# The hidden state's transposed, normalized copy: loaded and normalized in place instead of transposed on TensorE

## The chip, the cores and the metric

The kernel runs on one core of a Trainium2 chip. The metric is the device time of one execution in microseconds (us); the kernel before has a median of 1011.7 us over three runs (1010.71 to 1012.34).

## What is computed

One gated cross-attention block with a mixture feed-forward, in float32, for 8 batches of 256 tokens of width 512. In short:

```python
x = x + tanh(g_xattn) * attn(layernorm(x), ctx)   # q from [ctx, ln(x)], k and v from ln(x), ssm_k and ssm_v from ctx
x = x + tanh(g_ffn)   * ffn(layernorm(x))         # top-4 router over 128 experts, 8 gated bases, one shared expert
```

`layernorm` subtracts the mean of a token's 512 values and divides by the root of their variance + 1e-5. Queries, keys and values are matmuls that contract over the 512 features, so TensorE wants the normalized hidden state with the features on the partitions: x^T, 512 x 256 per batch, kept as a tile `xnT` of 128 partitions x 4 feature chunks x 256 tokens. The context `ctx` needs no norm and is already handed to the chip transposed.

## The kernel before, in words

**Rounds.** The work of a batch has three parts, and each round runs three batches side by side: `feed_forward(b)` of batch b, `attention(b + 1)` and `project(b + 2)` (the queries, keys and values). After the attention of a half (128 tokens) a `tail` does the output projection, the second norm, its transposes and the router. In the trace a full round takes about 121.8 us; rounds 0 to 5 hold a `project` of batches 2 to 7, and the last two rounds hold none.

**Who sets the order.** Nothing is reordered by hardware or a scheduler: every engine runs its instructions in the order in which Python issues them. Each part is a generator; `yield c` says "the next step of mine is due c units later", and `run` (L1251) always continues the generator that is due first. A round is 1.0 of this planned time. `project(b + 2)` starts at b + 0.01 (batch 2 at -0.06) and 60 of its units are 0.62 of a round (L1283), so one unit is 0.0103 round, nominally 1.26 us. `feed_forward(b)` starts at b, and 72.9 units are a round. `attention(b + 1)` starts at b - 0.2, and 74.1 units are 0.86 of a round.

**The feed-forward's pieces.** It goes through ten pieces of weights (8 bases, 2 shared). A piece is four groups of matmuls into a rotation of three PSUM banks: `one_and_five`, `four` of the piece before, `seven_and_six`, `two_and_three`, with the evictions between them on VectorE (DVE) and ScalarE (ACT): `first_tile` (L1084, L995), `mix_product` (L1113), `second_gate` (L1096), `keep_seven` (L1071 to L1075). Each group, once issued, loads the weights of the piece after next into the buffer that it has freed (`load_gu`, L349 and L351, on SyncE's queue, SP).

**The attention's steps.** `score` (L652) fills four PSUM banks; DVE adds the position bias and takes the row's bound (`soften`, L665); ACT takes exponentials (L684); GpSimd (POOL) divides (`divide`, L696); DVE transposes 32 x 32 blocks (`turn`, L709); TensorE multiplies by the values (L731). A later `score` reuses the four banks, so it follows the last `soften` on them.

**`project(b)` before.** It issues the loads of x and of the transposed context on SP (L112, L118; x has three buffers, so x of batch b waits until the result of batch b - 3 has been written out from the same buffer, L1183). 16 units later `norm` puts two `bn_stats`/`bn_aggr` pairs and an addition on DVE (L179 to L182) and one `pow` on POOL (L184); 3 units later DVE writes the two normalized tiles `xn` (L190); 3 units later the transposes begin. For each half of the tokens, `transposed` (L199) puts four 128 x 128 transposes on TensorE (L204) into the PSUM bank named `one`, and ACT copies them into `xnT` (L205). The bank `one` is shared with the tails: `hold` and `give` (L97 to L105) let one user in at a time, in the order of asking, with a gap of 0.007 round. Then come the keys (L532), the four query groups (L586) and the values (L606), each through the same bank. The tile `xnT` shares two buffers with the attention's `oT`. Batches 0 and 1 are projected by other code, with transposes.

Of the kernel before, what the change touches and what calls it, by code (L numbers as in the profile page):

```python
# [9 lines left out]
F32 = mybir.dt.float32  # L10
I32 = mybir.dt.int32
AF = mybir.ActivationFunctionType
ALU = mybir.AluOpType
AX = mybir.AxisListType

P = 128
B, T, HID = 8, 256, 512
NT = T // P
NC = HID // P
# [12 lines left out]
LN_EPS, EPS = 1e-5, 1e-8  # L32
# [5 lines left out]
def gated_block(  # L38
    ctx: ExitStack,
    tc: tile.TileContext,  # L40
    x: bass.AP,
    context_t: bass.AP,
    g_xattn: bass.AP,
    g_ffn: bass.AP,
# [17 lines left out]
    nc = tc.nc  # L62

    const = ctx.enter_context(tc.tile_pool(name="const", bufs=1))
    one = ctx.enter_context(tc.tile_pool(name="one", bufs=1))
    two = ctx.enter_context(tc.tile_pool(name="two", bufs=2))
    three = ctx.enter_context(tc.tile_pool(name="three", bufs=3))
    four = ctx.enter_context(tc.tile_pool(name="four", bufs=4))
    small = ctx.enter_context(tc.tile_pool(name="small", bufs=4))
# [4 lines left out]
    sums = ctx.enter_context(  # L74
        tc.tile_pool(name="sums", bufs=1, space=bass.MemoryType.DRAM)
    )
# [10 lines left out]
    def other_bank(n, name):  # L87
        return ps_gu.tile([P, 2 * T], F32, tag=f"gu{n}", name=name)
# [8 lines left out]
    def hold(gap=GAP):  # L97
        me = object()
        queue.append(me)
        while queue[0] is not me or now[0] < given[0] + gap:  # L100
            yield 0.4
# [6 lines left out]
    loaded = {}  # L108

    def load(b, eng=nc.sync):  # L110
        xt = three.tile([P, NT, HID], F32, tag="x", name=f"x_{b}")
        eng.dma_start(xt, x[b].rearrange("(t p) d -> p t d", p=P))  # L112
        return xt

    def load_context(b, eng=nc.sync):

        ctT = one.tile([P, NC, T], F32, tag="shT" if b == 1 else "ctT", name=f"ctT_{b}")
        eng.dma_start(ctT, context_t[b].rearrange("(c p) t -> p c t", p=P))  # L118
        return ctT
# [29 lines left out]
    neghalf = const.tile([P, NT], F32, tag="neghalf", name="neghalf")  # L149
# [23 lines left out]
    def norm(xt, tiles, name):  # L173

        n = len(tiles)
        stats = small.tile([P, NT, 6], F32, tag="stats", name=f"st_{name}")
        mv = small.tile([P, NT, 2], F32, tag="mv", name=f"mv_{name}")
        for j, t in enumerate(tiles):
            nc.vector.bn_stats(stats[:, j, :], xt[:, t, :])  # L179
            nc.vector.bn_aggr(mv[:, j, :], stats[:, j, :])  # L180
        veps = small.tile([P, NT], F32, tag="veps", name=f"ve_{name}")
        nc.vector.tensor_scalar(veps[:, :n], mv[:, :n, 1], LN_EPS, None, op0=ALU.add)  # L182
        rstd = small.tile([P, NT], F32, tag="rstd", name=f"rs_{name}")
        nc.gpsimd.tensor_tensor(rstd[:, :n], veps[:, :n], neghalf[:, :n], ALU.pow)  # L184

        def normed():
            xns = []
            for j, t in enumerate(tiles):
                xn = two.tile([P, HID], F32, tag="xn", name=f"xn_{name}_{t}")
                nc.vector.tensor_scalar(  # L190
                    xn, xt[:, t, :], mv[:, j, 0:1], rstd[:, j : j + 1],
                    op0=ALU.subtract, op1=ALU.mult,
                )
                xns.append(xn)
            return xns

        return normed

    def transposed(dst, src, t, name, bank):  # L199


        pt = bank([P, NC, P], f"tr_{name}_{t}")
        for c in range(NC):
            nc.tensor.transpose(pt[:, c, :], src[:, c * P : (c + 1) * P], ident)  # L204
        return lambda: nc.scalar.copy(dst[:, :, t * P : (t + 1) * P], pt)  # L205
# [127 lines left out]
    }  # L333

    summed = set()

    def load_gu(i, g):

        b, k = divmod(i, PIECES)
        if b >= B:  # L340
            return
        wgu[i, g] = ts = [
            two.tile([P, 2, I], F32, tag=f"w{g}{j}", name=f"w{g}{j}_{i}")
            for j in range(1 if g == 3 else 2)
        ]
        if g != 3 or k not in summed:
            of_bases, of_shared = ((w_gate, sw_gate), (w_up, sw_up))[(g - 1) // 2]
            src = of_bases[k] if k < NK else of_shared[k - NK]
            nc.sync.dma_start(ts[0], src[int(g in (2, 4))])  # L349
        if k in summed:  # L350
            nc.sync.dma_start(ts[-1], scratch[k, g])  # L351
# [16 lines left out]
    AFTER, BEFORE = 1.8, 0.8  # L368
# [132 lines left out]
    def put_values(pv):  # L501
# [2 lines left out]
            pv.rearrange("p t s (k d) -> p (t s) k d", d=D),  # L504
        )

    def project(b, xns=None):
        def own():
            yield from hold(0.0 if b == 1 else GAP)

        def bank(shape, name):
            return ps_one.tile(shape, F32, tag="one", name=name)

        free = give
        if b > 1:
            while b > 2 and b - 3 not in stored:
                yield 0.5
            loaded[b] = load(b), load_context(b)
            yield 16.0
        xt, ctT = loaded[b]  # L520
        if xns is None:
            normed = norm(xt, range(NT), f"a{b}")
            yield 3.0
            xns = normed()
            yield 3.0
        xnT = two.tile([P, NC, T], F32, tag="xo", name=f"xnT_{b}")
        kT = two.tile([P, 2, 2, T], F32, tag="kT", name=f"kT_{b}")

        def keys(pk, s):
            w_sb, src = ((wsk_sb, ctT), (wk_sb, xnT))[s]  # L530
            for c in range(NC):
                nc.tensor.matmul(  # L532
                    pk[:, s, :], lhsT=w_sb[:, c, :], rhs=src[:, c, :],
                    start=(c == 0), stop=(c == NC - 1),
                )

        if b == 1:

            yield BEFORE
            yield from own()  # L540
            pk = bank([P, 2, T], f"pk_{b}")
            for t in range(NT):
                if t:
                    yield BEFORE
                    keys(pk, 0)
                    yield MORE
                evict = transposed(
                    xnT, xns[t], t, f"x{b}",
                    lambda shape, name: other_bank(2, name).rearrange("p (c n) -> p c n", n=P),
                )  # L550
                yield AFTER
                evict()
            yield BEFORE
            keys(pk, 1)
            yield AFTER
        else:
            for t in range(NT):
                yield from own()
                evict = transposed(xnT, xns[t], t, f"x{b}", bank)
                yield AFTER - 0.8  # L560
                evict()
                free()
                yield BEFORE + 0.8
            yield from own()
            pk = bank([P, 2, T], f"pk_{b}")
            for s in range(2):
                keys(pk, s)
                yield AFTER

        for par in range(2):  # L570
            for s in range(2):
                nc.scalar.activation(
                    kT[:, par, s, :], pk[:, s, :], AF.Copy, scale=kmask[:, par : par + 1],
                )
        free()
        yield BEFORE
        if b == 1:
            yield BEFORE


        qT = two.tile([P, NB, G, Q], F32, tag="qT", name=f"qT_{b}")
        for g in range(G):
            yield from own()
            pq = bank([P, T], f"pq_{b}_{g}")
            for c in range(2 * NC):
                nc.tensor.matmul(  # L586
                    pq, lhsT=wq_sb[:, c, g * P : (g + 1) * P],
                    rhs=(ctT if c < NC else xnT)[:, c % NC, :],
                    start=(c == 0), stop=(c == 2 * NC - 1),
                )  # L590
                if c % NC == NC - 1:
                    yield MORE if c < NC else AFTER
            nc.scalar.activation(
                qT[:, :, g, :], pq.rearrange("p (b q) -> p b q", q=Q), AF.Copy, scale=-0.25
            )
            free()
            yield BEFORE
        projected[b] = kT, qT


        yield from own()
        pv = bank([P, NT, 2, HK * D], f"pv_{b}")
        for t in range(NT):
            for s, (w_sb, src) in enumerate(((wsv_sb, ctT), (wv_sb, xnT))):
                for c in range(NC):
                    nc.tensor.matmul(  # L606
                        pv[:, t, s, :], lhsT=src[:, c, t * P : (t + 1) * P], rhs=w_sb[:, c, :],
                        start=(c == 0), stop=(c == NC - 1),
                    )
            yield AFTER if t else MORE  # L610
        put_values(pv)
        free()
        yield BEFORE
# [671 lines left out]


_INS = [
    "x", "ctx_2048", "g_xattn", "g_ffn",
    "L0_xattn_Wq", "L0_xattn_Wk", "L0_xattn_Wv", "L0_xattn_Wsk", "L0_xattn_Wsv", "L0_xattn_Wo",
    "L0_ffn_w_router", "L0_ffn_w_gate", "L0_ffn_w_up", "L0_ffn_w_down",  # L1290
    "L0_ffn_amplitudes", "L0_ffn_expert_scale",
# [32 lines left out]
```

## Time and profile before

| | us |
|---|---|
| median of the runs | 1011.7 (1010.71 to 1012.34) |
| the profiled execution's own time | 1013.49 |
| its span in the trace | 1011.7 |
| mean granted TensorE clock | 0.993 |
| one full round (rounds 1, 2, 4, 5) | 121.7 to 121.8 |

The span is what the trace covers; the 1.8 us to the profiled execution's own time lie around it. Where the text speaks of a "view", it is one answer of the trace: the page with its busy shares; the groups (instructions by line, with count and mean duration); the timeline (instructions in order of start); the waits (who waited for whom); the chain of waits that ended last; and the busy time by stages, given by window. In the timeline the first column is the start and the second the time that the merged instructions span, both in us; a bracket gives the idle time before and what ended it. Matmuls are pipelined, so what a group costs TensorE is read from start to start, not from its busy time.

Other groups that are in play, from the same profile:

| line, engine | what | count | mean ns |
|---|---|---|---|
| L204 PE, tr_x | transposes of the hidden state, all batches | 64 | 289 |
| L205 ACT, xnT | their eviction | 16 | 583 |
| L190 DVE, xn_a | normalization, 128 x 512 | 16 | 571 |
| L179 DVE, st_a | statistics, 128 x 512 | 16 | 674 |
| L184 POOL, rs_a | power, 128 x 2 | 7 | 858 |
| L112 SP | load of x, 512 KB, six times | 6 | 4.8 us to landing |
| L118 SP | load of the context, 512 KB | 7 | 5.9 us to landing |

### The profile page before, as it was taken

How to read it: one execution, taken by the hardware profiler on the slowest of the kernel's cores; microseconds unless marked ns; L12 is line 12 of the kernel's file. 1: busy time of each engine (PE TensorE's matmuls, PEld its weight loads, DVE VectorE, ACT ScalarE, POOL GpSimd, SP SyncE). 2: the span in 40 equal slices, each digit the busy share in tenths (PEclk: the TensorE clock that was granted, in tenths of full speed). 3: DMA queues.
4: the chain of work that ended last, by engine and by line, in shares of the span. 5: the costliest groups of instructions: out<-in, count | busy, mean ns of one | idle time of the engine just before them, and what ended most of it. 6: DMA issues, size and time to landing. Idle time of an engine off the chain costs nothing.

```text
span 1011.7 us, 27844 instructions
## 1 busy us (share of the span) xinstructions
PE 985.7 (97%) x10470; PEld 797.3 (79%) x10470; DVE 601.8 (59%) x2241; ACT 441.6 (44%) x1657; POOL 471.6 (47%) x892
## 2 busy tenths in 40 slices
PE   8899799899999999999999999999999999999998
PEld 8777687768888687886778868797788868787885
DVE  2775767467553685536755467645756466665453
ACT  3754444246442564325543356423554245442231
POOL 4783676536542363423634246432455325651341
PEclk9999899999999999999999999999999999999999
DMA  6945744689354784457745586446954468665891
GB/s 208 219 171 155 224 152 129 185 216 304 124 164 144 208 288 142 147 166 217 249 127 158 167 256 216 135 137 190 276 188 140 150 181 260 201 192 167 281 301 64
DMA packets 117302, 192.15 MB, mean 190 GB/s; under 512 B 12848, under 2 KB 34864, under 8 KB 117168
## 3 DMA queue, kind: packets, MB, share of 16 engines
q1 hardware_dynamic: 112672, 184.87, 59.6%
q10 hardware_dynamic: 4112, 4.46, 1.3%
q8 instruction: 83, 1.36, 0.6%
q0 software_dynamic: 384, 1.05, 0.5%
q14 instruction: 51, 0.42, 0.1%
HBM read 158.87 MB, written 14.68 MB: 172 GB/s over the span
## 4 chain that ended last, share of the span: by engine, by line
PE 86%; DVE 5%; issue 2%; ACT 2%; POOL 2%; DMA 1%; SPq 1%; ACTq 0%; DVEq 0%; POOLq 0%
PE m L1028 39%; PE m L1037 10%; PE pq L586 8%; PE sc L731 6%; PE po L893 5%; PE sc L652 5%; PE pd L1171 4%; PE pk L532 2%; PE pv L606 2%; PE pd L1174 2%; PE pl L923 1%; DVE pr L665 1%; ACT pr L684 1%; PE tr_x L204 1%; SPq L496 1%
## 5 line engine op out<-in xcount | busy, mean ns | idle before, releaser
L696 POOL TENSOR_SCALAR pr<-pr,rd 128x192 f32<-128x192 f32 (+2 forms) x512 | 212.1, 434 | 243.9 <-DVE rd L693 226.8
L684 ACT ACTIVATE pr<-pr,nm 128x192 f32<-128x192 f32 (+2 forms) x512 | 219.0, 431 | 106.7 <-DVE nm L665 55.3
L1028 PE MATMUL m<-w,sT 128*128 128x256 f32 x1024 | 252.3, 380 | 1.3 <-issue 0.8
L1028 PEld LDWEIGHTS m<-w,sT 128*128 128x128 f32 x1024 | 193.6, 190 | 28.9 <-issue 1.5
L665 DVE CUSTOM_DVE_ANT_1 pr<-sc,nbias 128x192 f32<-128x192 f32 (+2 forms) x512 | 153.7, 321 | 98.0 <-PE sc L652 91.1
L1028 PE MATMUL m<-w,hT 128*128 128x256 f32 x768 | 203.8, 388 | 1.0 <-DVE u L1073 1.0
L1028 PEld LDWEIGHTS m<-w,hT 128*128 128x128 f32 x768 | 139.6, 191 | 25.6 <-issue 6.3
L1118 POOL TENSOR_TENSOR mixed<-mixed,th 128x256 f32<-128x256 f32 x112 | 81.5, 728 | 137.5 <-DVE th L1113 137.5
L709 DVE STREAM_TRANSPOSE pt<-pr 128x768 f32<-128x768 f32 (+2 forms) x128 | 111.4, 870 | 3.8 <-POOL pr L696 3.1
L684 ACT ACTIVATION_READ_ACCUMULATOR pr<-pr,nm 128x1 f32 x512 | 98.0, 191 | 0.0
L1074 POOL TENSOR_TENSOR m<-m,u 128x256 f32<-128x256 f32 x80 | 61.4, 768 | 67.3 <-DVE u L1073 58.5
L990 ACT ACTIVATE th<-m 128x256 f32<-128x256 f32 x80 | 30.7, 384 | 138.5 <-DVE up L1084 138.4
L731 PEld LDWEIGHTS sc<-pt,vbd 64*32 64x32 f32 x5120 | 60.6, 106 | 25.8 <-issue 14.2
L731 PE MATMUL sc<-pt,vbd 64*32 64x64 f32 (+2 forms) x5120 | 68.2, 228 | 8.9 <-DVE nm L665 5.3
L1096 DVE TENSOR_TENSOR gate<-u,m 128x256 f32<-128x256 f32 x80 | 33.2, 416 | 72.0 <-PE m L1028 66.5
L1084 DVE TENSOR_TENSOR up<-u,m 128x256 f32<-128x256 f32 x80 | 33.3, 416 | 67.9 <-PE m L1028 41.1
L990 ACT ACTIVATE th<-gate 128x256 f32<-128x256 f32 x80 | 33.3, 416 | 76.5 <-DVE gate L1096 76.5
L652 PE MATMUL sc<-kT,qT 32*128 32x192 f32 (+2 forms) x1024 | 63.6, 336 | 2.8 <-DVE nm L665 2.5
L1037 PE MATMUL m<-sT,w 128*128 128x128 f32 x512 | 66.2, 278 | 0.0
L652 PEld LDWEIGHTS sc<-kT,qT 32*128 32x128 f32 x1024 | 44.3, 184 | 26.5 <-issue 7.1
L1037 PEld LDWEIGHTS m<-sT,w 128*128 128x128 f32 x512 | 62.3, 194 | 0.4
L1171 PE MATMUL pd<-sd,shT 128*128 128x512 f32 x128 | 61.5, 603 | 0.2 <-DVE shT L1107 0.2
(131 smaller groups left out, 1376.0 us busy)
## 6 DMA issues: line engine op xcount, KB each, us to landing
w<-s SPq DMA_DIRECT2D x284, 256.0 KB, 3.5
w<-in_L_ffn_w_gate SPq DMA_DIRECT2D x130, 256.0 KB, 3.1
w<-in_L_ffn_w_up SPq DMA_DIRECT2D x73, 256.0 KB, 4.1
vbd<-vpad SPq DMA_DIRECT2D x120, 128.0 KB, 3.1
s<-w SPq DMA_DIRECT2D x40, 256.0 KB, 3.3
w<-in_L_ffn_shared_w_gate SPq DMA_DIRECT2D x32, 256.0 KB, 2.9
w<-in_L_ffn_shared_w_up SPq DMA_DIRECT2D x18, 256.0 KB, 3.8
sd<-in_L_ffn_shared_w_down SPq DMA_DIRECT2D x16, 256.0 KB, 3.5
```

The costliest lines, as they stand in the source:

```text
L586: nc.tensor.matmul(pq, lhsT=wq_sb[:, c, g * P : (g + 1) * P], rhs=(ctT if c < NC else xnT)[:, c % NC, :], start=(c == 0), stop=(c == 2 * N ...
L652: nc.tensor.matmul(seen(scs[p][:, j * COLS : (j + 1) * COLS], qb), lhsT=qT[rows, qb].rearrange("p g q -> p (g q)"), rhs=kT[rows, par, :, f ...
L665: nc.vector.tensor_tensor_reduce(out=part, in0=seen(scs[p][:, j * COLS : (j + 1) * COLS], qb0 + j), in1=bass.AP(tensor=bias.tensor, offset ...
L684: nc.scalar.activation(part, part, AF.Exp, bias=nmax, scale=-1.0, accum_out=den)
L696: nc.gpsimd.tensor_scalar(part, part, rden[:, p : p + 1], 1.0, op0=ALU.mult, op1=ALU.mult)
L709: nc.vector.transpose(pt[:, u % 4].rearrange("p c (s k) -> p (c s) k", s=2)[:, :, lo:], pr.rearrange("p c (s k) -> p (c s) k", s=2)[:, :, ...
L731: nc.tensor.matmul(scs[gp][32 * c : 32 * (c + 1), 2 * COLS + lo * Q : 2 * COLS + hi * Q], lhsT=vbd[rows, kb % (P // Q), kb // (P // Q) * 2 ...
L990: nc.scalar.activation(th, gate, AF.Tanh, scale=0.5)
L1028: nc.tensor.matmul(dst, lhsT=sides_of[m][c], rhs=w[:, c, :], start=(first and c == 0), stop=(c == NC // 2 - 1), skip_group_check=True,)
L1037: nc.tensor.matmul(dst[:, cols], lhsT=w[:, c, cols], rhs=sides_of[m][c], start=(first and ic == c == 0), stop=(c == NC // 2 - 1), skip_gro ...
L1118: nc.gpsimd.tensor_add(mixed[t], mixed[t], th)
L1171: nc.tensor.matmul(po, lhsT=shT[:, ic, t * P : (t + 1) * P], rhs=down[ic], **flags)
```

## The change

From batch 2 on, x is handed to the kernel a second time, transposed on the host. `xnT` is loaded with the raw x^T and normalized where it lies. The mean and the reciprocal deviation of a token are now needed along the free axis, the same on every partition; they are computed as before from x, written to a small DRAM tile `rows` (4-byte elements, 2 KB in all), and read back with a broadcast to all 128 partitions (`wide`, 256 KB). Then DVE subtracts the mean and POOL multiplies, in two halves of 128 x 512 each. The planned distances are new as well: 9 units from the loads to the statistics, 2 to the write, 8 to the read, 8 to the first half, and 2.1 after each half. The transposes, their evictions, and their two turns at the bank `one` are gone for batches 2 to 7. The scratch space for DMAs issued by POOL is set to 8192 bytes.

```diff
+    rows = {b: sums.tile([NT, 2, P], F32, tag=f"rows{b}", name=f"rows{b}") for b in range(2, B)}
...
+    def norm_transposed(b, xt, xnT):
+        stats = small.tile([P, NT, 6], F32, tag="stats", name=f"st_a{b}")
+        mr = small.tile([P, NT, 2], F32, tag="mv", name=f"mv_a{b}")
+        for t in range(NT):
+            nc.vector.bn_stats(stats[:, t, :], xt[:, t, :])
+            nc.vector.bn_aggr(mr[:, t, :], stats[:, t, :])
+        veps = small.tile([P, NT], F32, tag="veps", name=f"ve_a{b}")
+        nc.vector.tensor_scalar(veps, mr[:, :, 1], LN_EPS, None, op0=ALU.add)
+        nc.gpsimd.tensor_tensor(mr[:, :, 1], veps, neghalf, ALU.pow)
+        yield 2.0
+        nc.sync.dma_start(rows[b].rearrange("t s p -> p (t s)"), mr.rearrange("p t s -> p (t s)"))
+        yield 8.0
+        wide = one.tile([P, NT, 2, P], F32, tag="wide", name=f"wide_{b}")
+        nc.sync.dma_start(
+            wide.rearrange("p t s n -> p (t s n)"),
+            rows[b].rearrange("t s p -> (t s p)").partition_broadcast(P),
+        )
+        yield 8.0
+        for half in range(2):
+            part = xnT[:, half * NC // 2 : (half + 1) * NC // 2, :].rearrange(
+                "p c (t n) -> p c t n", t=NT
+            )
+            for which, eng, op in ((0, nc.vector, ALU.subtract), (1, nc.gpsimd, ALU.mult)):
+                row = wide[:, :, which, :]
+                eng.tensor_tensor(
+                    part, part,
+                    bass.AP(
+                        tensor=row.tensor, offset=row.offset,
+                        ap=[list(row.ap[0]), [0, NC // 2], [2 * P, NT], [1, P]],
+                    ),
+                    op,
+                )
+            yield 2.1
...
     def project(b, xns=None):
...
             loaded[b] = load(b), load_context(b)
-            yield 16.0
-        xt, ctT = loaded[b]
-        if xns is None:
-            normed = norm(xt, range(NT), f"a{b}")
-            yield 3.0
-            xns = normed()
-            yield 3.0
-        xnT = two.tile([P, NC, T], F32, tag="xo", name=f"xnT_{b}")
+            xnT = two.tile([P, NC, T], F32, tag="xo", name=f"xnT_{b}")
+            nc.sync.dma_start(xnT, x_t[b].rearrange("(c p) t -> p c t", p=P))
+            yield 9.0
+            xt, ctT = loaded[b]
+            yield from norm_transposed(b, xt, xnT)
+        else:
+            xt, ctT = loaded[b]
+            xnT = two.tile([P, NC, T], F32, tag="xo", name=f"xnT_{b}")
...
-            for t in range(NT):
-                yield from own()
-                evict = transposed(xnT, xns[t], t, f"x{b}", bank)
-                yield AFTER - 0.8
-                evict()
-                free()
-                yield BEFORE + 0.8
             yield from own()
             pk = bank([P, 2, T], f"pk_{b}")
...
-    nc = bacc.Bacc("TRN2", target_bir_lowering=False, num_devices=1)
+    nc = bacc.Bacc(
+        "TRN2", target_bir_lowering=False, num_devices=1, dynamic_dma_scratch_size=8192
+    )
...
-        if name == "ctx_2048":
+        if name in ("ctx_2048", "x_t"):
             a = a.transpose(0, 2, 1)
```

## The prediction

> **What bounds the kernel.** First the page's busy shares, then the busy time by stages, for round 2 (348.3 to 470.1).
>
> ```profile
> PE 985.7 (97%) x10470; PEld 797.3 (79%) x10470; DVE 601.8 (59%) x2241; ACT 441.6 (44%) x1657; POOL 471.6 (47%) x892
> ```
>
> ```profile
> core 0: us, PE busy (x) PEld busy (x) DVE busy (x) ACT busy (x) POOL busy (x), PEclk, DMA share, GB/s
> 348.30:470.10 121.80, 121.47 (x1303) 98.39 (x1299) 72.58 (x278) 55.01 (x206) 52.62 (x103) 1.00 0.61 188
> ```
>
> ```profile
> 355.40:364.60 9.20, 9.20 (x177) 7.61 (x176) 6.49 (x28) 5.44 (x22) 4.62 (x10) 1.00 0.99 351
> 364.60:373.70 9.10, 9.09 (x60) 7.47 (x59) 9.00 (x35) 5.67 (x23) 6.15 (x11) 1.00 0.91 293
> 373.70:382.50 8.80, 8.80 (x113) 7.46 (x112) 5.78 (x25) 4.48 (x18) 6.62 (x13) 1.00 0.49 160
> ```
>
> TensorE is the bound: busy 121.47 of 121.80 us, clock 1.00, and the chain of waits that ended last lies 86% on it. Matmul time taken away is gained in full, unless an engine beside it is late. In 355 to 374 two are near their limit: the DMA engines (0.99, 351 GB/s) and DVE (9.00 of 9.10 us).
>
> **Removed on TensorE.** The timeline of round 2 shows what four transposes cost from start to start.
>
> ```profile
> 371.58 0.60 PE L204 MATMUL tr_x<-ident,xn_a 128*128 128x128 f32 x4
> 372.02 1.03 PE L1028 MATMUL m<-w,hT 128*128 128x256 f32 x4
> 373.06 0.65 PE L204 MATMUL tr_x<-ident,xn_a 128*128 128x128 f32 x4
> 373.65 0.60 PE L652 MATMUL sc<-kT,qT 32*128 32x192 f32 x7
> ```
>
> The first four take 372.02 - 371.58 = 0.44. The four L1028 behind them need 0.86 (the same form goes from 369.86 to 370.72), so TensorE is free for the second four at 372.88 and is done with them at 373.65: 0.77, of which 0.17 are put down to DVE. I count 0.44 + 0.60 = 1.04 per batch; 0.44 + 0.77 = 1.21 is the most, 2 x 0.44 = 0.88 the least. In round 0 the pairs start at 121.93, 122.37 and 125.05, 125.55: 0.94. Five rounds and that: 5 x 1.04 + 0.94 = **6.1 us gained** (5.3 to 7.0).
>
> The Trainium skill speaks against the change here: "VectorE: DVE Perf Modes", The three transpose paths, gives TensorE 390 ns for a 128 x 128 transpose (bf16) and warns of a DMA that transposes by strides. By that figure 48 transposes would be an estimated 18.7 us, three times what the starts show; I go by the starts. The strided DMA is not at issue for x, which the host transposes; no run here shows it.
>
> **Moved: the statistics.** This is the step I fear. One unit is 0.62/60 = 0.0103 round. Before, the statistics stand at 0.01 + 16 x 0.0103 = 0.175 round, now at 0.01 + 9 x 0.0103 = 0.103. In the feed-forward's units that is 0.103 x 72.9 = 7.5. Adding its yields, `mix_product(0, 0)` stands at 1.73 + 1.73 + 0.6 + 1.13 + 0.6 + 1.13 = 6.92 and `second_gate(0)` at 7.78; the attention's steps (0.0116 round each from -0.2) put a `soften` and a `turn` at 0.102. So on DVE the statistics now stand behind the `turn` at 357.35 and ahead of the gate at 358.48. The check on this arithmetic: 0.175 gives 12.8, behind the `silu2` at 11.84, and there the trace has them (364.18).
>
> ```profile
> 354.51 0.38 SPq L112 DMA_DIRECT2D x<-in_x  x1
> ```
>
> The view of L112 in this window gives its landing, and the timeline the DVE instructions (those between are left out):
>
> ```profile
> DMA to landing us min/median/max: 4.8/4.8/4.8
> ```
>
> ```profile
> 357.35 0.44 DVE L709 STREAM_TRANSPOSE pt<-pr 128x256 f32<-128x256 f32 x1
> 358.48 0.42 DVE L1096 TENSOR_TENSOR gate<-u,m 128x256 f32<-128x256 f32 x1 [0.69 <-PE m L1028]
> ...
> 362.96 0.42 DVE L1084 TENSOR_TENSOR up<-u,m 128x256 f32<-128x256 f32 x1 [0.99 <-PE m L1028]
> ...
> 363.57 0.35 DVE L665 CUSTOM_DVE_ANT_1 pr<-sc,nbias 128x192 f32<-128x192 f32 x1
> ...
> 364.18 0.69 DVE L179 BATCH_NORM_STATS2 st_a<-x 128x6 f32<-128x512 f32 x1
> ```
>
> The load of x is not earlier: on SP it waits for the result of batch b - 3 to leave its buffer. It lands at 354.51 + 4.8 = 359.3, but DVE gets to the statistics at 357.8. **A new wait**: DVE stands still for 1.5 us, then the statistics take 1.8 (364.18 to 366.0), and the gate comes at 361.1 instead of 358.5, 2.6 late. Behind it queue gate, `soften`s, `silu2`, the eviction sum `u`, and behind the gate ACT's tanh. Rounds 1 to 5, landing (issue + 4.5 to 4.8) plus 1.8 minus the old start of the gate: 2.0, 2.6, 1.7, 1.7, 2.8, sum 10.8.
>
> TensorE waits for this at the next `score` (364.57), whose banks the `soften` at 363.57 frees (done 363.85; its bank is the last of four filled, at about 364.9, so 1.0 of slack). DVE also idles for 0.98, 0.99, 1.95, 0.98, 0.99 ahead of L1084 (the bracket), which takes up delay; ACT's turn in the loop (tanh, a copy, then `u`, which today starts 0.11 after that copy) adds an estimated 0.35. So TensorE loses 2.0 + 0.35 - 0.98 - 1.0 = 0.4, then 1.0, 0, 0.1, 1.2: **2.7 us lost** (0 if DVE's order differs, 10.8 if nothing takes it up). Without the statistics and `xn` in 364 to 374, DVE has 2.8 us to catch up there.
>
> Round 0: by the same arithmetic (and round 0's start at about -0.13) the statistics come before L1084 at 103.53, and x lands at 102.35 + 4.8 = 107.15: that DVE instruction is up to 107.15 + 1.8 - 103.5 = 5.4 late. But the chain of waits there stands still for a weight load (5.53 us, until 111.95) and has the statistics behind it on DVE (1.75); the wait falls ahead of that stop and the 1.75 leave it. I take 0, with -1.8 and +3.6 as ends.
>
> **Added, and what covers it.**
> - DVE: two subtractions at 0.82 (L980's DVE row, same shape) for two L190 at 0.54: +0.6 per batch, at 0.289 and 0.311 round, about 375 to 380, where DVE is idle 2.6 of the stage's 8.8 us (at 380.92). Cost 0; without cover 0.6 x 6 = 3.6.
> - POOL: two multiplications at 1.29 (L980's POOL row). In front of `divide` they delay a `turn` that follows about a step of four later; POOL idles 1.9 ahead of the `divide` at 381.81. The second half of the keys wants the product 3.9 units (4.9 us) later. Cost 0; without cover 2.6 x 6 = 15.5, and in round 0, where POOL is busiest (71.8 of 122), I allow 1.
> - ACT loses two copies of 0.58 per batch.
> - SP: x^T (issue 0.46, like L118), `rows`, `wide`. The weight loads behind come 0.5 later and share the DMA engines with 0.5 MB more, 1.5 us at 351 GB/s. They are issued for the piece after next, some 12 us ahead (issued 357.35, used 369.86). `rows` waits for the `pow`, and weight loads wait behind it for about 1 us: covered as well. Without cover, 1.5 x 6 = 9.
> - `rows` to landing: no row shows 4-byte writes to DRAM. Nearest are L250's kind, 4-byte rows into SBUF at the start: 5.4 and 6.5, and 9.0 us for the expert scale; below, the vbd loads' 3.1. `wide` is issued 8 units (10 us) later, so all but the longest are hidden; the longest would hold SP's queue, not TensorE. `wide` has another 8 units. Cost 0.
> - The Trainium skill ("DMA: Bandwidth & Descriptors", Specifications) says that transfers under 512 B are read-modify-written and gives about 2.0 us fixed; by that alone the round trip would be an estimated 4 us, inside its 16 units. No run here shows it yet.
> - The keys stand at 0.332 instead of about 0.29 round, so the first queries fall behind the tail's output projection in the line for bank `one` instead of ahead of it. The line is two turns shorter, TensorE has other work queued: 0, with 2 us either way.
> - POOL's halved scratch: eight DMAs at the start use it. 0; 5.0 (their landing) if they had to wait for one another.
>
> **Sum.** 6.1 - 2.7 = 3.4 less. The profiled execution, 1013.5, becomes 1010.1; it lies 1.8 above the median, and the median becomes 1011.7 - 3.4 = **1008.3**.
>
> **Rivals.**
> - *All hidden* (0.15): DVE's delay never reaches a `score`. For it: DVE is idle 40% of the span. Against: 9.00 of 9.10. 1011.7 - 6.1 = 1005.6, with 7.0 gained 1004.7.
> - *Nothing left* (0.15): the new line for bank `one` or POOL returns the rest, another 3 us: 1011.5.
> - *Slower* (0.2): the wait of DVE for x passes into TensorE. Price 10.8 + 3.6 - 6.1 = +8.3, 1020.0; it decides from where more than 6.1 of the 14.4 pass, that is 1.0 per round instead of my 0.5. For it: DVE runs in order and feeds ACT, POOL and TensorE in the same step. Against: the idle times in the brackets. Its middle is 1016.
>
> **How the numbers follow.** Forecast 0.5: 1006 to 1011, of which 0.43 below 1009.7. A measurement tells 0.2%, 2.0 us. Faster: 0.15 + 0.43 = 0.58. Same: 0.07 + 0.12 = 0.19. Slower: 0.2 + 0.03 = 0.23. The range drops the best end of the hidden case and the worst of the slower one: 1004 to 1017.
>
> **What would show it.** L179 `st_a` waits for `DMA x` about 1 to 2 us in rounds 1 to 5 and up to 4 in round 0; `score` L652 waits for DVE about 1 us in rounds 2 and 5; rounds take about 121.3; no subtraction waits for `wide`; TensorE's busy time falls by about 6. I am wrong if rounds grow, if a key matmul waits for POOL, or if a round's gain comes or goes behind 0.35 round.

## The result and the profile after

| | before | after |
|---|---|---|
| median, us | 1011.9 (1010.71 to 1012.34) | 1036.9 (1034.52 to 1040.21) |
| profiled execution, span | 1013.49, 1011.7 | 1034.52, 1032.7 |
| five rounds, from the first load of x (L112, now L113) to the sixth | 618.8 | 637.6 |

After stands to before as 1.0263, 95% interval 1.0239 to 1.0287: 25 us slower, where 3.4 less was forecast. It lies above the range (1004 to 1017).

The busy shares of the page after, as on the page before:

```profile
PE 983.3 (95%) x10422; PEld 789.2 (76%) x10422; DVE 609.4 (59%) x2241; ACT 437.6 (42%) x1645; POOL 492.4 (48%) x904
```

TensorE does 48 transposes less (10422 instead of 10470) and is busy 2.4 us less, but it stands still for 23 us more. Round 2 by the busy time of its stretch (load of x to load of x):

```profile
361.36:488.38 127.02, 122.31 (x1292) 98.01 (x1291) 73.83 (x277) 54.41 (x205) 56.06 (x106) 0.99 0.65 185
```

It idles for 4.7 of 127.0 us, where the row of before had 0.3 of 121.8. The chain of waits, 86% on TensorE before, now has a tenth in DMAs:

```profile
PE 75%; DMA 11%; DVE 5%; SPq 3%; issue 3%; POOL 2%; ACT 1%; DVEq 0%; POOLq 0%; ACTq 0%
```

Which engine TensorE waits for is in the waits of after (total us, times, longest):

```profile
PE sc L761 <- DVE nm L695: 15.8, 10, 2.9
PE m L1058 <- DVE th L1025: 9.0, 2, 7.0
PE pq L616 <- DVE x L928: 4.6, 5, 0.9
```

In the kernel before, the first of these lines reads 5.3, 1, 5.3: one stop in round 0, where the changed kernel has the 7.0 of the second line instead. Behind round 0 the first line holds 15.4 us in nine waits, and the kernel before has none there.

And what DVE waits for, in the same view:

```profile
DVE xnT L534 <- DMA wide<-rows: 17.6, 5, 4.1
DVE st_a L514 <- DMA x<-in_x: 8.7, 5, 5.5
```

The second line is the wait that the prediction feared. The first one is the wait that it said there would not be. The chain of waits, round 2 (start, us, what):

```profile
368.89 12.39 DMA rows<-mv_a
...
381.31 6.69 DMA wide<-rows
```

The write of 2 KB takes 12.4 us to land and the read of it 6.7; the plan had 8 units (10 us) for each. (`wide`, which follows the landing, is issued 9.0 to 13.1 us behind the write in the six rounds.) From there the wait reaches TensorE: the timelines of DVE and of TensorE, and the busy time of the stretch behind the stop.

```profile
388.02 0.69 DVE L534 TENSOR_TENSOR xnT<-xnT,wide 128x512 f32<-128x512 f32 x1 [3.54 <-DMA wide<-rows]
389.44 1.27 PE L761 MATMUL sc<-pt,vbd 64*32 64x96 f32 x64 [2.56 <-DVE nm L695]
390.20:393.50 3.30, 3.30 (x45) 2.70 (x36) 3.22 (x10) 1.43 (x7) 3.22 (x5) 0.50 0.68 250
```

In rounds 1 to 5 this stop of TensorE takes 2.8, 2.6, 1.2, 2.2 and 2.9 us, 11.6 of the 15.4. With the three longest, in rounds 1, 2 and 5, the granted clock falls to 0.50 for 6.8, 3.4 and 3.4 us. TensorE is busy for 12.7 us of that; if this work took half as long at the full clock, 6.3 us went with it, an estimate of the most.

Between the write and the read, SP stands still (timeline of SP, its fifth to eighth DMA behind the write; `w<-s` is merged, x2):

```profile
373.66 0.33 SPq L351 DMA_DIRECT2D w<-in_L_ffn_w_up  x1
380.37 0.89 SPq L353 DMA_DIRECT2D w<-s  x2
381.31 0.42 SPq L523 DMA_DIRECT2D wide<-rows  x1
```

In the program each of SP's DMAs waits until the one eight places ahead of it has landed (the records name eight semaphores, which the DMAs take in turn). The one issued at 380.37 waits for a weight load issued at 366.73, two us *before* the write: 13.6 us to landing, where these loads have a median of 3.5 in the kernel before. A load lands in 16 parts; 15 of this one's came after 5.9 to 6.1 us, and only the last was late. The five loads issued behind the write, from 369.98 to 373.66, took 10.2 to 11.5 us. What the DMA engines do meanwhile is in the DMA view from 364 to 392, in 40 slices of 0.7 us: the busy share in tenths, and the GB/s moved.

```profile
DMA  9999999999999999558968884469999899999999
GB/s 395 382 388 347 354 367 386 395 372 392 392 375 304 387 199 26 9 12 59 61 126 102 108 117 50 61 222 401 401 375 225 152 389 418 401 395 410 386 386 383
```

From 374 to 382 the engines are four to nine tenths busy and move 9 to 126 GB/s instead of 380. In the packet records the 512 pieces of 4 bytes start between 372.7 and 373.3, and the 43 packets of 1 KB and more that start between 374 and 376 take 1.2 us on average instead of 0.05 to 0.09.

### The profile page after: what moved, and what is told of

Read it like the earlier page. It is cut to its first block, busy times and chain, and to the rows that moved or that the text cites. A ratio compares the mean times of both kernels' runs of the same rounds, so it can differ in the third digit from the quotient of the medians.

```text
span 1032.7 us, 27793 instructions
## 1 busy us (share of the span) xinstructions
PE 983.3 (95%) x10422; PEld 789.2 (76%) x10422; DVE 609.4 (59%) x2241; ACT 437.6 (42%) x1645; POOL 492.4 (48%) x904
## 4 chain that ended last, share of the span: by engine, by line
PE 75%; DMA 11%; DVE 5%; SPq 3%; issue 3%; POOL 2%; ACT 1%; DVEq 0%; POOLq 0%; ACTq 0%
PE m L1058 28%; PE m L1067 10%; PE pq L616 8%; PE pd L1201 5%; PE sc L761 5%; PE po L923 5%; PE sc L682 3%; DMA wide<-rows 3%; PE pd L1204 3%; DMA rows<-mv_a 2%; PE pv L636 2%; DMA x<-in_x 2%; PE pk L569 2%; SPq L498 2%; DMA out<-x 1%
## 5 line engine op out<-in xcount | busy, mean ns | idle before, releaser
L726 POOL TENSOR_SCALAR pr<-pr,rd 128x192 f32<-128x192 f32 (+2 forms) x512 | 214.8, 437 | 208.3 <-DVE rd L723 184.2
L1058 PE MATMUL m<-w,sT 128*128 128x256 f32 x1024 | 256.1, 384 | 10.1 <-DVE th L1025 9.0
L1058 PEld LDWEIGHTS m<-w,sT 128*128 128x128 f32 x1024 | 196.0, 192 | 39.8 <-DVE th L1025 9.8
L1148 POOL TENSOR_TENSOR mixed<-mixed,th 128x256 f32<-128x256 f32 x112 | 84.8, 757 | 140.6 <-DVE th L1143 140.4
L761 PE MATMUL sc<-pt,vbd 64*32 64x96 f32 (+2 forms) x5120 | 71.3, 229 | 17.2 <-DVE nm L695 15.8
L682 PEld LDWEIGHTS sc<-kT,qT 32*128 32x128 f32 x1024 | 42.7, 185 | 26.4 <-issue 10.2
L682 PE MATMUL sc<-kT,qT 32*128 32x192 f32 (+2 forms) x1024 | 60.7, 335 | 1.3 <-DVE nm L695 0.9
L1105 POOL TENSOR_TENSOR m<-m,m 128x256 f32<-128x256 f32 x80 | 58.9, 737 | 6.3
```

What stands on the lines that cost most here:

```text
L682: nc.tensor.matmul(seen(scs[p][:, j * COLS : (j + 1) * COLS], qb), lhsT=qT[rows, qb].rearrange("p g q -> p (g q)"), rhs=kT[rows, par, :, f ...
L726: nc.gpsimd.tensor_scalar(part, part, rden[:, p : p + 1], 1.0, op0=ALU.mult, op1=ALU.mult)
L761: nc.tensor.matmul(scs[gp][32 * c : 32 * (c + 1), 2 * COLS + lo * Q : 2 * COLS + hi * Q], lhsT=vbd[rows, kb % (P // Q), kb // (P // Q) * 2 ...
L1058: nc.tensor.matmul(dst, lhsT=sides_of[m][c], rhs=w[:, c, :], start=(first and c == 0), stop=(c == NC // 2 - 1), skip_group_check=True,)
L1148: nc.gpsimd.tensor_add(mixed[t], mixed[t], th)
```

## The experiments

Theories. **W**: the write in 4-byte pieces chokes the DMA engines; weight loads and the wide read come late, and DVE, then TensorE, wait. **X**: DVE's wait for x at the early statistics. **T**: the traffic of x^T. **L**: the later place of keys and queries in the line for bank `one`. Later **G**: the gain for the transposes was not to be had. The kernel before ran beside each group, with medians from 1009.9 to 1010.9 (1007.1 to 1014.1); ratios are to these runs. The groups ran apart, so runs of two groups are best compared by their ratios.

### The write

**The write alone, in the kernel before**, 2 units after the statistics:

```diff
-            yield 3.0
+            yield 2.0
+            nc.sync.dma_start(
+                rows[b].rearrange("t s p -> p (t s)"), normed.mv.rearrange("p t s -> p (t s)")
+            )
+            yield 1.0
```

> The kernel before, plus one thing: behind each norm of batches 2 to 7 the statistics are written to a small DRAM tile in 4-byte pieces, as the change does it; nothing reads them. Theory W (the write): 512 pieces of 4 bytes hold the DMA engines' queues for some 8 to 12 us (in the changed kernel the write lands 12.4 us after its issue in round 2), and the weight loads behind it come late: 3 to 15 us slower than before (1015 to 1027), with SP standing still behind the write in every round. Theory X (VectorE's wait for x at the early statistics), theory L (the line for the bank called one, and the shifted order) and theory T (the traffic of x^T): none of these is in this kernel, so the time is that of before within 2 us.

1021.8, ratio 1.0094 (1.0062 to 1.0125), as W said: 11.9 us by the medians, 9.5 by the ratio. SP waits for weight loads up to 6.5 us, though at four places and not in every round, with nothing of the change but the write in the kernel:

```profile
SPq L353 <- DMA w<-s: 14.5, 4, 6.5
```

**The same numbers in runs of 16 bytes**, in the kernel after: `rows` and `wide` hold the four values of a partition side by side, and the subtraction reads with a stride.

```diff
+    rows = {b: sums.tile([P, NT, 2], F32, tag=f"rows{b}", name=f"rows{b}") for b in range(2, B)}
...
+        nc.sync.dma_start(rows[b].rearrange("p t s -> p (t s)"), mr.rearrange("p t s -> p (t s)"))
```

> The changed kernel, but the statistics are written as one run of 16 bytes per partition (128 pieces instead of 512) and read back in that order; VectorE and GpSimd then pick them with a stride. Theory W: the write lands in about 3 to 5 us, wide is issued when it was planned, VectorE no longer waits for it: 1005 to 1015. Theories X, L and T: none of their causes is touched, so it stays near 1037 (at most 4 us less).

1013.6, ratio 1.0045 (1.0026 to 1.0063): one edit takes back 22 of the 25 us. No subtraction waits any more, TensorE's waits for DVE at the value matmuls behind round 0 fall from 15.4 to 4.3 us, and the write lands as follows:

```profile
DMA to landing us min/median/max: 3.5/5.0/6.1
```

**No write** (the wide read fetches 2 KB of x^T instead, so the numbers it normalizes with are not the statistics):

```diff
-        nc.sync.dma_start(rows[b].rearrange("t s p -> p (t s)"), mr.rearrange("p t s -> p (t s)"))
...
+            x_t[b, :2, :].rearrange("a n -> (a n)").partition_broadcast(P),
```

> The changed kernel without the write; wide reads 2 KB of the input instead, so the result is not normalized by the right numbers. Theory W: the whole loss is gone, 1004 to 1013, at or a little below the kernel with 16-byte runs. Theories X, L and T: near 1037.

1012.8, ratio 1.0026 (1.0008 to 1.0043). The wide read as such costs little.

**The 4-byte write from ScalarE's queue**, in the kernel after:

```diff
-        nc.sync.dma_start(rows[b].rearrange("t s p -> p (t s)"), mr.rearrange("p t s -> p (t s)"))
+        nc.scalar.dma_start(rows[b].rearrange("t s p -> p (t s)"), mr.rearrange("p t s -> p (t s)"))
```

> The kernel after with the 4-byte write issued by ScalarE's queue in place of SyncE's. If the loss comes from SyncE's queue standing still behind the slow write (its weight loads and the wide read in order behind it): most of it goes, 1012 to 1020 us. If the write chokes the DMA engines themselves, whichever queue issues it: 1030 to 1040 us, and the wide read still lands late.

1049.8, ratio 1.0380 (1.0353 to 1.0407): slower still, above both expectations. Changing the queue does not help: the write lands 11.9 to 13.0 us after its issue and SP still waits, now for the write itself (the waits of SP), since the program counts DMAs of both queues in one turn of eight:

```profile
SPq L353 <- DMA rows<-mv_a: 43.6, 5, 10.6
```

So this run does not separate SP's stop from the choke by its time alone; its records do. The nine packets of SP's queue that start between 377 and 378, two us after the write's pieces, take 2.6 us on average instead of 0.05 to 0.09, and the three weight loads that SP issues behind the write, on the other queue, take 11.2 to 11.5 us.

**Number or size of the pieces**, each added to the kernel before as in the first run: 128 pieces of 16 bytes (`rows` laid out as in the second run), and 128 pieces of 4 bytes (`rows[...][:, 0:1]`, one mean per partition).

> The kernel before with a write of the statistics in 128 pieces of 16 bytes that nothing reads. If the number or the size of the pieces is what makes the 4-byte write slow: within 3 us of the kernel before (512 pieces of 4 bytes cost 11.9), landing in about 5 us. If any small write does it: 8 to 14 us more.

1010.7, ratio 1.0001 (0.9982 to 1.0019): nothing. The landing in this kernel:

```profile
DMA to landing us min/median/max: 1.4/4.1/4.5
```

> The kernel before with a write of 128 pieces of 4 bytes (one mean per partition) that nothing reads. If the number of pieces sets the price: about a quarter of the 512 pieces' 11.9 us, 1 to 4 us more, landing in 5 to 7 us. If the size of a piece sets it: 8 to 14 us more, landing in 10 to 12 us.

1017.0, ratio 1.0055 (1.0035 to 1.0074), 6.1 more. The landing:

```profile
DMA to landing us min/median/max: 8.3/8.9/9.4
```

Neither answer alone: a quarter of the pieces costs half of 11.9. With the same 128 pieces, 4 bytes against 16 is 8.9 against 4.1 us to landing and 6.3 us of the kernel's time; four times as many pieces of 4 bytes cost another 5.8. Size and number both count; why small pieces are slow is not shown.

### The load of x^T and the statistics

**The load of x^T in the kernel before**, at the start of the round, into the tile that the transposes then fill:

```diff
+            xnT = two.tile([P, NC, T], F32, tag="xo", name=f"xnT_{b}")
+            nc.sync.dma_start(xnT, x_t[b].rearrange("(c p) t -> p c t", p=P))
```

> The kernel before, plus the load of x^T (512 KB) into the tile xnT behind the loads of x and of the context; the transposes' evictions then overwrite it. Theory T: the weight loads behind it are late, 3 us or more above before. Theories W, X and L: the time of before within 2 us, since weights are loaded some 12 us ahead.

1014.8, ratio 1.0052 (1.0036 to 1.0068): T, not what the others expected. The runs of this kernel have a granted clock of 0.990 to 0.992, those of before 0.991 to 0.996; at the same clock, 0.991, they take 1014.7 to 1015.5, those of before 1012.5 to 1014.1, so 1 to 2 us of the 4.9 are left. In round 0 a weight load is awaited for 1.82 us instead of 0.48, ahead of TensorE's longest stop, and the clock is lower behind it (0.90 instead of 1.00 from 120 to 130). That this is the way of the loss is not shown: it is read from one profile each, and these two executions took 1013.1 us with the load and 1013.5 without it.

**Later statistics, later x^T, both** (all three on the version with 16-byte runs: statistics at 16 units with distances of 4.5 and 4.5; x^T issued behind the wide read; both, with x^T behind the write):

```diff
-            yield 9.0
+            yield 16.0
...
-        yield 8.0
+        yield 4.5
```

> The version with 16-byte runs of the statistics, with the statistics of a round 16 units behind its start in place of 9, and shorter distances behind them, so that the keys stay at their place. X (VectorE's wait for x at the early statistics costs what the trace shows as the step of TensorE behind it): 3 to 7 us less than the version with 16-byte runs, 1007 to 1011 us, and the waits of L514 on x near 0. T (the traffic of x^T) and L (the line for bank one): unchanged within 2 us.

> The version with 16-byte runs, with the load of x^T moved from the start of the round to right behind the wide read, 10 units later; the statistics stay at 9 units. T (the x^T load delays the x and weight loads around it): 2 to 5 us less than the version with 16-byte runs, 1008.5 to 1011.5 us. X and L: unchanged within 2 us.

> The version with 16-byte runs with both moves: statistics at 16 units, the x^T load right behind the write of the rows at 18. X and T together: 1004 to 1010 us, the fastest of these and at or below the kernel before. If neither X nor T is a cause: within 2 us of the version with 16-byte runs.

1024.6 (1.0129, 1.0102 to 1.0156), 1016.3 (1.0060, 1.0034 to 1.0085), 1023.8 (1.0131, 1.0088 to 1.0173). All three miss. In the first the waits for x are gone, and the wait for the round trip, too short now, has come in their place; part of it turns up again at TensorE's value matmuls:

```profile
DVE xnT L534 <- DMA wide<-rows: 12.8, 5, 3.6
```

```profile
PE sc L761 <- DVE nm L695: 12.8, 6, 5.2
```

That both lines say 12.8 is chance: TensorE's holds the stop of 5.2 us in round 0 that the kernel before has too (5.3). The other 7.5 us, in five waits, compare with 4.3 in the version with the statistics at 9. So the two runs with late statistics cannot price X, but they show the round trip's need: distances of 4.5 units are 12.8 / 5 = 2.6 us per round too short, and part of what is missing is taken from TensorE. The move of x^T alone brought nothing at the one other place that was tried, where the subtraction waits 2.6 us for x^T itself.

**Statistics at 13**, distances 6 and 6, the keys where they were (the same diff with 13.0, 6.0, 6.0):

> The version with 16-byte runs, with the statistics 13 units behind the start of the round in place of 9 and 6 units from the write to the read and from the read to the first subtraction in place of 8; the keys stay at their place. X (VectorE's wait for x at the early statistics is what is left of the loss): 3 to 6 us less than the version with 16-byte runs (1013.6), 1008 to 1011, and no subtraction waits for the wide read. If the round trip needs more than 6 units, the subtraction waits 0.5 us or more per round and the time is not less. L: unchanged within 2 us.

1012.8, ratio 1.0021 (1.0003 to 1.0039): 0.8 us less than with the statistics at 9 by the medians and 2.4 by the ratios, whose intervals overlap. The waits for x fall from 6.5 to 1.0 us in all, while 4.2 us of waits for the wide read come up. X is a real wait with a small price here; these runs don't separate it from 0.

### The gain

**No transposes in the kernel before**: ScalarE copies the normalized tile instead.

```diff
-                evict = transposed(xnT, xns[t], t, f"x{b}", bank)
+                evict = lambda: nc.scalar.copy(
+                    xnT[:, :, t * P : (t + 1) * P], xns[t].rearrange("p (c n) -> p c n", n=P)
+                )
```

> The kernel before with the 48 transposes on TensorE of batches 2 to 7 left out: the copies to x^T take the normalized x as it stands, so the output is not the reference's; everything else is kept. It prices the gain alone. If TensorE's time for transposes is gained in full: 5.3 to 7.0 us less than the kernel before. If another engine or a transfer sets the end of these stretches: within 2 us of the kernel before.

1011.0, ratio 1.0005 (0.9989 to 1.0021): none of the 6.1 us (the interval leaves 1.1 at most). The timeline of round 2, where the prediction shows the transposes:

```profile
370.88 0.59 PE L654 MATMUL sc<-kT,qT 32*128 32x192 f32 x4
371.83 1.19 PE L654 MATMUL sc<-kT,qT 32*128 32x192 f32 x12 [0.36 <-DVE nm L667]
372.95 0.89 PE L733 MATMUL sc<-pt,vbd 64*32 64x96 f32 x64
```

Counted from the first keys of round 1, TensorE is at this `score` after 117.05 us (118.16 in the kernel before), waits there for DVE's `soften`, and starts the value matmuls behind it after 119.12 in both kernels; the next keys come after 121.77 in both. The transposes had filled that wait. The `soften` that ends this wait stands at the same distance from those keys in both kernels (its last instruction starts after 117.87 and 117.88 us): DVE sets the pace. In this stretch it is busy 11.85 of 12.40 us (361.0 to 373.4).

**No norm at all** in the kernel after (no statistics, round trip, subtraction or product):

```diff
-            yield 9.0
+            yield 27.0
             xt, ctT = loaded[b]
-            yield from norm_transposed(b, xt, xnT)
```

> The kernel after with the whole norm of batches 2 to 7 left out: no statistics, no write, no wide read, no subtraction and no multiplication, so the output is not the reference's; x, the context and x^T are loaded as they are, and the keys stand at 0.29 of a round. It prices the most that the change could have brought. If the removed transposes are time on TensorE's path once VectorE is free of the norm: 4 to 7 us less than the kernel before. If another wait fills their place, as in the run without transposes: within 2 us of it.

1011.3, ratio 1.0006 (0.9990 to 1.0022). Here the `score` no longer waits, and the same microsecond is lost 26 us later, in each round, at the queries behind the tail's sum:

```profile
394.90 1.99 PE L615 MATMUL pq<-ctT,wq 128*128 128x256 f32 x8 [0.97 <-DVE x L927]
```

**No transposes and no norm in the kernel before**, the turns at bank `one` kept:

```diff
-            normed = norm(xt, range(NT), f"a{b}")
-            yield 3.0
-            xns = normed()
-            yield 3.0
+            yield 6.0
+            xns = [xt[:, t, :] for t in range(NT)]
```

> The kernel before with the transposes, the statistics and the normalization of batches 2 to 7 left out (ScalarE copies the raw x into x^T, so the output is not the reference's); every turn at bank one and every planned distance is kept. If VectorE's load of statistics and normalization was what TensorE waited for once the transposes were gone: 4 to 7 us less than the kernel before. If the line for bank one or another wait sets the round: within 2 us of it.

1003.1, ratio 0.9921 (0.9894 to 0.9949): 7.8 less. With DVE's statistics and `xn` gone the `score` comes at once (round 2, start to start 0.87), and the bank order is as before:

```profile
365.87 0.94 PE L652 MATMUL sc<-kT,qT 32*128 32x192 f32 x16
366.74 0.89 PE L731 MATMUL sc<-pt,vbd 64*32 64x96 f32 x64
```

The three runs together fit this reading: the transposes' time counts only where DVE is relieved at the same place **and** the line for bank `one` stays as it was. The change moves DVE's work and changes the line. Two things are not separated: no run leaves out the norm and keeps the transposes, so how much of the 7.8 us is the transposes' is open, and the run with no norm also loads x^T, which the one with 7.8 us does not.

### The line for bank `one`

**Keys 4 units earlier** (16-byte runs, statistics at 9, distances 6 and 6):

> The version with 16-byte runs, with 6 units in place of 8 in both distances, so that the keys stand 4 units earlier, at 0.29 of a round as in the kernel before; the statistics stay at 9 units. L (the later place in the line for bank one costs 0.9 us in each round): 3 to 5 us less than the version with 16-byte runs, and the queries' wait for VectorE at the tail's sum is gone. X: unchanged within 2 us.

1027.7, ratio 1.0174 (1.0146 to 1.0202). The queries' wait is gone, as L said, and the time is 14 us more, which it did not say. DVE waits 7.6 us for the wide read and 6.9 for x, and TensorE waits 11.4 us for DVE at the `score`, in twelve waits (0.9 in two with the keys later). That is not all of the 14 us; what makes up the rest is open.

**A wider gap**: 0.016 of a round instead of 0.007 ahead of each turn of the projection, on the version with the statistics at 13, and alone in the kernel before.

```diff
-            yield from hold(0.0 if b == 1 else GAP)
+            yield from hold(0.0 if b == 1 else 0.016)
```

> The version with 16-byte runs and the statistics at 13 units, with a gap of 0.016 of a round in place of 0.007 ahead of each turn of the projection at bank one, so that the queries are issued behind the tail's sum. L (the queries' wait for that sum, 0.9 us per round): 3 to 5 us less than the version with the statistics at 13 units (1012.8), 1007.5 to 1010, and that wait is gone. If another wait takes its place: within 2 us of it or more.

> The kernel before with the gap of 0.016 of a round ahead of each turn of the projection at bank one in place of 0.007, and nothing else. If the gap helps only where the change had put the queries ahead of the tail's sum: within 2 us of the kernel before, or slower. If the gap helps by itself: 2 to 5 us less, and the version with the wider gap then owes nothing to the change.

With the change 1008.6, ratio 0.9968 (0.9950 to 0.9986): the queries' wait is gone and the time 4.1 less than with the statistics at 13 (5.4 by the ratios), as L expected. But the gap alone in the kernel before gives 1002.9, ratio 0.9929 (0.9908 to 0.9950), the fastest kernel of this study. The faster version thus owes nothing to the change; with the same gap the change still costs 4 (by the ratios) to 6 us (by the medians). In the kernel with the gap alone TensorE is busy 979.0 us with the same 10470 matmuls (985.7 before), and rounds 1 to 4 take 119.9 to 122.0 (121.1 to 123.0 before, each from load of x to load of x); which turn gives this was not taken apart. The busy shares of its page:

```profile
PE 979.0 (98%) x10470; PEld 791.8 (79%) x10470; DVE 600.1 (60%) x2241; ACT 438.9 (44%) x1657; POOL 472.5 (47%) x892
```

**Two units more for the wide read**, on the version with the gap:

> The version with 16-byte runs, statistics at 13 units and the wider gap (1008.6), with 8 units in place of 6 from the wide read to the first subtraction. If the wait of the subtraction for the read (5.4 us in all) passes into TensorE: 2 to 5 us less, 1004 to 1007, and that wait is gone. If it is hidden: within 2 us, or more where the later keys meet another turn in the line.

1020.6, ratio 1.0108 (1.0074 to 1.0141). It does not answer its question. The projection had become too late: in round 2 ScalarE copies the values of the next batch at 462.65, after half of them had been read for the attention at 454.90, and before the other half at 466.92, so half of the values are those of the batch before; and it waits 6.1 us for the first reads. In the version with the gap and distances of 6 the copy stands at 453.30 and the reads at 456.76: 3.5 us of room are left of the 21.9 in the kernel before.

## Why the prediction was wrong

- **"`rows` to landing ... all but the longest are hidden; the longest would hold SP's queue, not TensorE. ... Cost 0."** This step failed. The landing was bounded at 3.1 to 9.0 by rows of loads into SBUF and took 12.4 in round 2. Worse, it was weighed as the latency of one transfer, and it disturbs the others: the five loads issued behind it took 10.2 to 11.5 us, where such loads have a median of 3.5. Alone it costs 11.9 us (9.5 by the ratio); with the wide read, whose wait passes from DVE into TensorE (11.6 us of stops in rounds 1 to 5, and a lower clock with three of them), 22 of the 25. "No subtraction waits for `wide`" was named as the sign, and it failed (17.6 us).
- **"Matmul time taken away is gained in full"**, 6.1 us. Failed too: 0 in the kernel before. The clue was in the row that I showed: DVE 9.00 of 9.10 beside TensorE's 9.09, and 0.17 us behind the second transposes that I put down to DVE and did not follow. Two engines were at their limit there, and taking work from one of them gained nothing.
- **DVE's wait for x**, 2.7 lost. The mechanism was right: waits of 0.3 to 1.3 us in four later rounds. They are shorter than the 1 to 2 us forecast, and one of the five rounds has none. Round 0 has the longest, 5.5 where up to 4 was forecast, and it reaches TensorE (`m` waits 7.0 us for `th`). But the kernel before stands still there as well: from 100 to 130 TensorE waits 8.9 us in the changed kernel, 5.4 in the version with 16-byte runs and 5.7 before. So the 0 taken for round 0 holds without the 4-byte write, and 3.2 is the most with it. The price of all these waits is small once the write is gone: 0.8 to 2.4 us between statistics at 9 and at 13, not told from 0.
- **x^T, "covered"**, cost 0. 4.9 us measured in the kernel before, 1 to 2 of it at the same clock; by what path stays open. A term that was mis-sized, inside the 9 that I gave without cover.
- **The line for bank `one`**, "0, with 2 us either way". The queries wait 0.9 us in each of five rounds, 4.6 in all, and a wider gap gives 4.1 to 5.4 back. Mis-sized; the order of turns proved worth more than the change (7.9 us in the kernel before).
- By the runs: the write and what hangs behind it 22 us, the line 4, x^T up to 4.9, the waits for x 0.8 to 2.4, the gain 0 alone and 7.8 together with the norm. They overlap and don't add up to 25.
- The subtractions and products and the smaller scratch: no run takes one of them out alone, so their 0 is neither shown nor refuted.
- **The rivals.** "Slower" got the sign, by another mechanism: I put the wait into DVE for x; it was DVE for the wide read. None of the rivals had a transfer that slows the others.
- The Trainium skill, as quoted in the prediction ("DMA: Bandwidth & Descriptors", Specifications), says that transfers below 512 bytes are read-modify-written. Its about 2.0 us fixed stand in another section of that page, Anatomy of one DMA — SWDGE (gpsimd) path, which is on DMAs issued by GpSimd; this write is issued by SP. The direction of the first holds for the 4-byte write (8.9 us for 128 pieces, 12.4 for 512), not for the 16-byte one, which is below 512 too, lands in 4.1 and costs nothing that the runs can tell. The estimate of 4 us for the round trip was 19.1 in round 2 (12.4 + 6.7).

## What to carry to other kernels

Price a small DMA not by its own landing but by what it does to the loads in flight beside it, and give each partition's values as one run: 16 bytes in place of 4 x 4 took back 22 us here. Before counting removed matmul time as gain, look whether a second engine is as full in the same few microseconds: here it was, and the time went into the next wait. Where turns at a shared bank are planned by hand, vary the gap alone first; here it was worth more than the change.

## What the runs showed of the hardware

- Sizes of a write to DRAM, issue to landing: 512 pieces of 4 bytes 12.4 us (round 2 of the changed kernel; 11.9 to 13.0 from ScalarE's queue), 128 of 4 bytes 8.9, 128 of 16 bytes 4.1 to 5.0 (medians). While the 512 pieces are under way the engines' throughput falls from about 380 GB/s to between 9 and 126 for about 8 us.
- The spread between runs of one kernel goes with the granted clock: the kernel before takes 1007.1 to 1010.1 at 0.996 and 1012.5 to 1014.1 at 0.991, about 1 us per 0.001. Whether the clock or the stops behind it make the time is not separated. The clock falls with a stop of TensorE: from 110 to 120 of the kernel before, with a stop of 5.25 us, the row of this stretch shows 4.26 us busy and a clock of 0.66.

```profile
110.00:120.00 10.00, 4.26 (x73) 3.24 (x73) 7.84 (x26) 2.61 (x11) 5.28 (x6) 0.66 0.44 164
```

From 118 to 120 TensorE is busy without a gap again, and the clock is still 0.50. The Trainium skill ("TensorE: Matmul & The Clock Gate", What's actually happening) says that an idle window of about 3.4 us throttles TensorE to half. The half agrees; the length differs. In the changed kernel stops of 2.56, 2.80 and 2.88 us were enough for 0.50, and in the version with 16-byte runs one of 2.10; stops of 1.23 and 2.16 us went without. So a stop costs more than its length: the 64 value matmuls behind the stops of 2.80 and 2.88 took 1.55 us, where they take 0.89 in round 2 of the kernel before.
